# Attention with layers woven into it: three resident images, more buffers, later sums, depthwise taps through ScalarE, full-array projections

## The chip, the cores and the metric

One core of a Trainium2 chip. The metric is the device time of one execution in microseconds (us), as the median of the runs. The kernel before takes 3923 us. Here single runs of one kernel agree within 0.25%, and where a ratio is given it comes from three or more rounds in which both kernels ran on the same chip. The experiments ran in four batches on different chips; the kernel before had medians from 3921.2 to 3924.0 us in them, so a few us between runs of different batches mean nothing.

Engines are named as in the profile: PE is TensorE, PEld its weight loads, DVE is VectorE, ACT is ScalarE, POOL is GpSimd, SP is SyncE. "L643" is line 643 of the kernel named.

## The reference, cut to what matters

Four images of 256 channels and 48x48 points pass through four layers. Each layer is added to its input and works on the group norm of it. The attention of layer 0 (8 heads) and layer 2 (one head) over all 2304 points is most of the work.

```python
# layer 0: attention with normed q and k; the norm runs over the points
q, k, v = split(einsum('oc,bchw->bohw', w_qkv, x))       # 8 heads of 64
q = l2norm_over_points(q); k = l2norm_over_points(k)
attn = softmax(einsum('bhdi,bhdj->bhij', q, k) * 10.0)   # 2304 x 2304 a head
out = w_out @ einsum('bhij,bhdj->bhid', attn, v) + b_out

# layer 1: a gate from a depthwise filter on a 16 x 16 grid
t = blur_pool(max_pool_3x3(x), stride=3)                 # 48x48 -> 16x16
s = dwconv(t, w_h1) + dwconv(t, w_v1) + diag1(t, w_h2) + diag2(t, w_v2)   # 81 different taps
out = x * upsample(sigmoid(batch_norm(s)))

# layer 2: a non-local block with 64 channels
f = einsum('bnc,bcm->bnm', theta(x), phi(x)) * 64 ** -0.5
out = batch_norm_over_the_batch(W @ einsum('bnm,bmc->bnc', softmax(f), g(x)))

# layer 3: channel gates, depthwise 3x3, instance norm, leaky relu
x = x + layer_i(group_norm(x))                           # for each of the four
```

## The kernel before

The scores are worked out transposed: 128 keys on the partitions (a key block), 384 queries (a slice) of two heads beside each other. A **unit** is one slice of two heads: 18 key blocks in nine **groups** of two. A **stretch** is one pair of heads of one image in layer 0: six units, 54 groups; in layer 2 a stretch is one image: three units, 27 groups. There are 16 stretches and then four.

```python
    ppool = main.enter_context(tc.tile_pool(name="pt", bufs=5))      # exponentials
    apool = main.enter_context(tc.tile_pool(name="acc", bufs=2))
    hpool = main.enter_context(tc.tile_pool(name="half", bufs=2))    # half sums and rows
    ...
    def quarters(outs, lhsT, rhs, start, stop):      # four 64x64 matmuls for one 128x128
        for c in HALVES:
            for r, out in zip(HALVES, outs):
                nc.tensor.matmul(out[c], lhsT=lhsT[r, c], rhs=rhs[r], start=start, stop=stop)

    def join(out, ab, bias):                         # adds the two halves of the rows
        nc.scalar.activation(out, ab[0], AF.Identity, bias=bias)
        nc.vector.tensor_add(out, ab[1], out)

    def scores(u, j):
        ps = sc_tile()
        ...                                          # four matmuls of 64x64 on 384 columns
        pt = ppool.tile([P, 2, SL], F32, tag="pt", name="pt")
        nc.scalar.activation(pt, ps[:, :, :SL], AF.Exp, scale=u["scale"])

    def add_up(u, g):                                # softmax sums over the key blocks
        pts = [u["pt"][j] for j in range(g * G, (g + 1) * G)]
        if g in u["paired"]:                         # some groups: POOL adds the two blocks first
            half = hpool.tile([P, 2, SL], F32, tag="half", name="half")
            nc.gpsimd.tensor_add(half, pts[0], pts[1])
        ...
        for term in ready:
            nc.vector.tensor_add(u["acc"], u["acc"], term)

    def total(u):                                    # sums over the 128 partitions of acc
        ab = [pj_tile()[:, :SL] for _ in range(2)]
        ...                                          # four matmuls of ones with u["acc"]
        row = hpool.tile([P, 2, SL], F32, tag="half", name="row")
        for i in range(2):
            nc.scalar.copy(row[:, i, :], ab[i])
        ...                                          # DMA of the row to other partitions

    # groups from a unit's end until its sums, fold, 1/sum, division, and what follows
    AT_TOTAL, AT_FOLD, AT_INVERT, AT_DIVIDE, AT_AFTER = 1, 2, 4, 8, 11
```

The loop gives each engine its instructions in this order, group by group. Every engine works through its own list in order.

```python
        for t, (u, g, st) in enumerate(groups):
            for j in range(g * G, (g + 1) * G):
                scores(u, j)                # matmuls, and the exponentials of ACT
            if prev is not None:
                add_up(*prev)
            do(due, t)
            do(fills, t)                    # projections of the next pair, total(), outputs
            for lane in st["others"]:
                ...                         # the next "ticks" of layer 1 and of the group norms
            if prev is not None:
                ...                         # weigh(): attention times v for the group before
                if pg == NG - 1:
                    last(pu, t)             # copies the unit's result, enters its work in due, fills
```

Layer 1 of an image is a generator cut into ticks by `yield`; image 3's runs beside layer 2.

```python
        for i, (dr, dc) in enumerate(TAPS):          # 81 taps, three a tick
            ...
            nc.vector.scalar_tensor_tensor(acc, src, w, acc, ALU.mult, ALU.add)
            if i % TAPS_A_TICK == TAPS_A_TICK - 1 or i == len(TAPS) - 1:
                yield
    ...
        if b > 0:                                    # layer 2, image b, 27 groups
            spread(work, stats(b - 1, 1), [2, 3])    # two matmuls into two pj buffers each,
            spread(work, stats(b - 1, 2), [11, 12])  # then bn_stats by DVE
        if b + 1 < B:
            spread(work, stats(b, 0), [20, 21])
```

Small PSUM results all go through two buffers, called pj.

## Time and profile before

| | us |
|---|---|
| time, median of 4 runs (3918.99 to 3924.59) | 3923.0 |
| profiled execution | 3922.4 |
| prologue, to the first exponential | 74.1 |
| four stretches without layer 1 beside them (177.3 to 181.3 each) | 719.4 |
| twelve stretches with layer 1 (189.4 to 200.6 each) | 2337.2 |
| layer 2, first three images (135.5, 140.2, 168.5) | 444.2 |
| layer 2's last image and the tail | 347.2 |

A stretch is taken from the copy of the pair's last raw result (the product of attention and v, copied out of PSUM) to the next such copy; bounds are good to some 0.5 us (the first exponential starts at 74.4 us). These are groups of the kernel before (line, engine, operation, operands, count, then busy us and mean ns of one, then idle time before them):

```profile
L285 DVE TENSOR_TENSOR acc<-acc,pt 128x768 f32<-128x768 f32 x792 | 941.9, 1189 | 62.5 <-ACT pt L245 1.9
L643 DVE SCALAR_TENSOR_TENSOR l1acc<-pd,grid,l1acc 128x256 f32<-128x256 f32 x640 | 464.3, 726 | 16.4
```

And these are its waits over the whole run (what waited, for what, us in total, times, longest):

```profile
PEld pj L292 <- DVE acc L285: 144.4, 93, 7.8
PE pj L292 <- DVE acc L285: 98.7, 65, 6.9
ACT pt L245 <- DVE acc L285: 46.2, 42, 3.3
ACT pt L245 <- DVE acc L279: 18.7, 23, 2.3
```

104 units take their sums in this way; at 93 of them the weight load of the sums stood waiting for DVE's additions, and PE itself waited 98.7 us there. PE's next longest wait, of the scores for ACT, is 32.5 us in sum.

### The profile page before, as it was taken

Reading aid. Unit: us, or ns where it says so; the run is one execution under the profiler, and the core shown is the slowest. Engines: PE = TensorE matmul, PEld = TensorE weight load, DVE = VectorE, ACT = ScalarE, POOL = GpSimd, SP = SyncE. Lnnn points to the kernel's source line nnn. Section 1 sums busy time; section 2 is a strip of 40 time slices with the busy share of each in tenths; the row PEclk is TensorE's granted clock in tenths of the full one; section 3 lists DMA queues with packets and bytes.
Section 4 is the critical chain, followed back from the end, with each engine's and each line's share of the span. In section 5 each row is a group of like instructions: output and inputs, shape, how many; then the busy total and the mean of one; then the engine's idle time right before and its main releaser. Section 6 shows DMA issues by size and latency. Waiting matters only on the chain.

```text
span 3922.4 us, 91105 instructions
## 1 busy us (share of the span) xinstructions
PE 3595.0 (92%) x38642; PEld 1743.8 (44%) x38642; DVE 2947.4 (75%) x3799; ACT 2119.7 (54%) x3317; POOL 1450.9 (37%) x874
## 2 busy tenths in 40 slices
PE   6999999999989999999899999999999997869785
PEld 3444444444444444444444444444444443324343
DVE  2566555568987897689888976897888778874687
ACT  3656565656555555555565555555655543434353
POOL 1333333334333333343343333334433454553232
PEclk9999999999999999999999999999999998889897
DMA  4111111111111111111111111111110000000001
GB/s 149 20 28 21 25 20 28 19 27 24 20 17 26 17 27 23 20 24 20 20 24 20 23 24 20 24 20 24 20 16 8 8 4 5 5 5 5 1 25 73
DMA packets 109872, 91.10 MB, mean 23 GB/s; under 512 B 56096, under 2 KB 106896, under 8 KB 107664
## 3 DMA queue, kind: packets, MB, share of 16 engines
q1 hardware_dynamic: 106688, 84.06, 11.9%
q8 instruction: 305, 5.00, 0.5%
q10 hardware_dynamic: 2768, 1.14, 0.1%
q14 instruction: 111, 0.91, 0.1%
HBM read 54.62 MB, written 9.44 MB: 16 GB/s over the span
## 4 chain that ended last, share of the span: by engine, by line
PE 54%; DVE 33%; issue 6%; ACT 4%; POOL 3%; DMA 1%; SPq 0%; DVEq 0%; ACTq 0%; POOLq 0%
PE av L259 18%; PE sc L239 18%; DVE acc L285 14%; DVE l1acc L643 6%; PE pj L226 6%; PE pj L527 3%; PE pj L497 3%; PE pj L292 2%; DVE sc L1086 2%; POOL half L270 1%; DVE av L1086 1%; ACT pt L245 1%; DVE gn_st L168 1%; ACT k L229 1%; DVE k L230 1%
## 5 line engine op out<-in xcount | busy, mean ns | idle before, releaser
L245 ACT ACTIVATE pt<-sc 128x768 f32<-128x768 f32 x1944 | 1482.6, 809 | 1099.7 <-PE sc L239 936.9
L270 POOL TENSOR_TENSOR half<-pt 128x768 f32<-128x768 f32 x477 | 978.1, 2051 | 2098.7 <-ACT pt L245 1891.4
L239 PE MATMUL sc<-q,k 64*64 64x384 f32 x13824 | 1291.2, 486 | 17.3 <-ACT pt L245 15.0
L259 PE MATMUL av<-pt,v 64*64 64x384 f32 x13824 | 1299.2, 488 | 4.7 <-ACT raw L328 4.7
L285 DVE TENSOR_TENSOR acc<-acc,pt 128x768 f32<-128x768 f32 x792 | 941.9, 1189 | 62.5 <-ACT pt L245 1.9
L239 PEld LDWEIGHTS sc<-q,k 64*64 64x64 f32 x13824 | 529.3, 134 | 625.3 <-issue 521.7
L259 PEld LDWEIGHTS av<-pt,v 64*64 64x64 f32 x13824 | 522.5, 134 | 609.1 <-issue 593.8
L285 DVE TENSOR_TENSOR acc<-acc,half 128x768 f32<-128x768 f32 x459 | 480.6, 1047 | 68.5 <-POOL half L270 65.5
L643 DVE SCALAR_TENSOR_TENSOR l1acc<-pd,grid,l1acc 128x256 f32<-128x256 f32 x640 | 464.3, 726 | 16.4
L531 DVE SCALAR_TENSOR_TENSOR x<-pj,bo,x 128x384 f32<-128x384 f32 x192 | 118.5, 617 | 265.9 <-PE pj L527 265.4
L226 PE MATMUL pj<-xs,w 64*64 64x384 f32 x3072 | 292.5, 488 | 5.7 <-ACT q L229 4.1
L239 PE MATMUL sc<-qv,kd 64*64 64x384 f32 x1728 | 189.8, 505 | 17.7 <-ACT pt L245 17.6
L259 PE MATMUL av<-pt,qv 64*64 64x384 f32 x1728 | 199.5, 525 | 6.6 <-ACT raw L328 6.6
L292 PE MATMUL pj<-acc,ones 64*64 64x384 f32 x832 | 97.5, 529 | 99.6 <-DVE acc L285 98.7
L226 PEld LDWEIGHTS pj<-xs,w 64*64 64x64 f32 x3072 | 119.2, 134 | 142.9 <-issue 126.5
L527 PE MATMUL pj<-o,wo 128*128 128x384 f32 x384 | 158.8, 517 | 18.5 <-DVE bias L460 11.0
L497 PEld LDWEIGHTS pj<-w,xs 128*128 128x128 f32 x1152 | 137.1, 193 | 54.3 <-issue 42.4
L497 PE MATMUL pj<-w,xs 128*128 128x128 f32 x1152 | 155.1, 285 | 4.0 <-ACT k L229 4.0
L230 DVE TENSOR_TENSOR k<-pj,k 128x384 f32<-128x384 f32 x96 | 53.3, 555 | 139.5 <-ACT k L229 137.4
L336 POOL TENSOR_TENSOR o<-o,rinv 128x384 f32<-128x384 f32 x95 | 137.9, 1451 | 0.0
L230 DVE TENSOR_TENSOR q<-pj,q 128x384 f32<-128x384 f32 x96 | 53.4, 557 | 111.0 <-ACT q L229 111.0
L239 PEld LDWEIGHTS sc<-qv,kd 64*64 64x64 f32 x1728 | 79.4, 139 | 96.7 <-issue 54.7
(207 smaller groups left out, 2759.9 us busy)
## 6 DMA issues: line engine op xcount, KB each, us to landing
xs<-in_x_dram SPq DMA_DIRECT2D x96, 384.0 KB, 3.1
rinv<-rinv SPq DMA_DIRECT2D x208, 94.5 KB
x<-in_x_dram SPq DMA_DIRECT2D x8, 1152.0 KB, 5.5
out_dram<-x SPq DMA_DIRECT2D x6, 1152.0 KB, 4.3
l<-row SPq DMA_DIRECT2D x416, 1.5 KB, 1.8
w<-in_wqkv_dram SPq DMA_DIRECT2D x32, 192.0 KB, 6.7
rinv<-ls SPq DMA_DIRECT2D x208, 1.5 KB, 1.7
out_dram<-x SPq DMA_DIRECT2D x6, 384.0 KB, 2.6
```

The lines of the kernel that those rows point to most:

```text
L226: nc.tensor.matmul(out[c], lhsT=lhsT[r, c], rhs=rhs[r], start=start, stop=stop)
L230: nc.vector.tensor_add(out, ab[1], out)
L239: nc.tensor.matmul(ps[c * D : (c + 1) * D, h, :SL], lhsT=u["of"]["k"][r, j0 : j0 + D], rhs=u["of"]["q"][r, u["qc"]], start=True, stop=True,)
L245: nc.scalar.activation(pt, ps[:, :, :SL], AF.Exp, scale=u["scale"])
L259: nc.tensor.matmul(u["av"][h * D : (h + 1) * D, half, :SL], lhsT=value(u, j, h)[r], rhs=pt[r, h, :], start=j == 0, stop=j == JB - 1,)
L270: nc.gpsimd.tensor_add(half, pts[0], pts[1])
L285: nc.vector.tensor_add(u["acc"], u["acc"], term)
L292: nc.tensor.matmul(out[c], lhsT=ones[r], rhs=u["acc"][r, h, :], start=True, stop=True)
L336: eng.tensor_mul(o, o, u["rinv"])
L497: nc.tensor.matmul(ps[:, i * P : (i + 1) * P], lhsT=xs[s][:, k, i * P : (i + 1) * P], rhs=at["w"][:, k, 2, :], start=k == 0, stop=k == NK - 1,
L527: nc.tensor.matmul(ps[:, :SL], lhsT=wo[:, p, k * P : (k + 1) * P], rhs=o, start=True, stop=True)
L643: nc.vector.scalar_tensor_tensor(acc, src, w, acc, ALU.mult, ALU.add)
```

## The change

Its intent: take the waits for DVE off PE's path. Six things are done together.

- Ten buffers of exponentials instead of five, and three of half sums instead of two. The room comes from holding three images on the chip instead of four: image 3 takes the tile of image 0, which is written to DRAM and fetched back for layer 2's projection and for the tail.
- The sums of a unit are taken three groups after its end instead of one, and what follows moves with them.
- Layer 1's 81 taps: ACT makes the products, DVE adds up to five of them in one reduction.
- q, k and layer 2's theta and phi are projected with 128 rows and columns at once, so no join; q, k and v of a slice come in one group.
- Weights and norms of the next pair are fetched and made earlier.
- 48 small border copies of layer 1 move from ACT to DVE (`nc.scalar.copy` becomes `nc.vector.tensor_copy`; those after the normalising stay on ACT), and a few more ticks stand before steps that cross to another engine.

The diff, cut to its core:

```diff
-    X = [xpool.tile([P, NK, N], F32, tag=f"x{b}", name=f"x{b}") for b in range(B)]
+    NX = B - 1
+    X = [xpool.tile([P, NK, N], F32, tag=f"x{b}", name=f"x{b}") for b in range(NX)]
+    X.append(X[0])
+    x_out = dram.tile([P, NK, N], F32, name="x_out")
...
-    ppool = main.enter_context(tc.tile_pool(name="pt", bufs=5))
+    ppool = main.enter_context(tc.tile_pool(name="pt", bufs=10))
-    hpool = main.enter_context(tc.tile_pool(name="half", bufs=2))
+    hpool = main.enter_context(tc.tile_pool(name="half", bufs=3))
...
-    AT_TOTAL, AT_FOLD, AT_INVERT, AT_DIVIDE, AT_AFTER = 1, 2, 4, 8, 11
+    AT_TOTAL, AT_FOLD, AT_INVERT, AT_DIVIDE, AT_AFTER = 3, 2, 6, 10, 11
...
         def qk(s, t):
-            ab = [pj_tile()[:, :SL] for _ in range(2)]
+            ps = pj_tile()[:, :SL]
             for k in range(NK):
-                quarters(ab, at["w"][:, k, t, :], xs[s][:, k, :], k == 0, k == NK - 1)
-            join(to[:, cols], ab, at["bias"][:, t : t + 1])
+                nc.tensor.matmul(
+                    ps, lhsT=at["w"][:, k, t, :], rhs=xs[s][:, k, :],
+                    start=k == 0, stop=k == NK - 1,
+                )
+            nc.scalar.activation(to, ps, AF.Identity, bias=at["bias"][:, t : t + 1])
...
-    TAPS_A_TICK = 3
-    L1_TICKS = 2 * 8 + -(-len(TAPS) // TAPS_A_TICK) + 1 + 3
+    NT = 4
+    ROUNDS = [range(0, NT + 1)] + [
+        range(i, min(i + NT, len(TAPS))) for i in range(NT + 1, len(TAPS), NT)
+    ]
+    L1_TICKS = 2 * 10 + 2 * len(ROUNDS) + 2 + 3
...
+        bufs = [
+            lp.tile([P, L1_BUF], F32, tag=tag, name="prod").rearrange("p (n s) -> p n s", s=NT + 1)
+            for tag in ("t1", "t2")
+        ]
+        def products(n):
+            for i, t in enumerate(ROUNDS[n]):
+                ...
+                nc.scalar.activation(
+                    bufs[n % 2][:, :, min(n, 1) + i].rearrange("p (r c) -> p r c", c=AS),
+                    pd[:, PAD + dr : PAD + dr + AS, PAD + dc : PAD + dc + AS],
+                    AF.Identity, scale=grid[:, k, g : g + 1],
+                )
+        products(0)
+        yield
+        for n, taps in enumerate(ROUNDS):
+            last = n == len(ROUNDS) - 1
+            if not last:
+                products(n + 1)
+                yield
+            to = acc.rearrange("p r c -> p (r c)") if last else bufs[(n + 1) % 2][:, :, 0]
+            nc.vector.tensor_reduce(
+                to, bufs[n % 2][:, :, : min(n, 1) + len(taps)], AX.X, ALU.add
+            )
+            yield
...
+        if (b, p) == (2, 0):
+            for s in range(NSL):
+                work.setdefault(s, []).append(lambda s=s: send(s))         # image 0 to DRAM
+                work.setdefault(s + 8, []).append(lambda s=s: receive(s))  # image 3 into its tile
```

Note the product's place: `p (n s)` with `s` the five summands, so the five terms of one point lie beside each other, and ACT writes every fifth element, **20 bytes apart**. Layer 1 of an image has 146 ticks instead of 110.

## The prediction

> **What bounds the kernel now.** I read the page first. TensorE (PE) is busy for 92% of the span, so at first sight nothing but fewer matmuls can help. But the chain that ended last gives a third of the span to VectorE (DVE):
>
> ```profile
> PE 3595.0 (92%) x38642; PEld 1743.8 (44%) x38642; DVE 2947.4 (75%) x3799; ACT 2119.7 (54%) x3317; POOL 1450.9 (37%) x874
> PE 54%; DVE 33%; issue 6%; ACT 4%; POOL 3%; DMA 1%; SPq 0%; DVEq 0%; ACTq 0%; POOLq 0%
> ```
>
> So I cut the span into stages: the prologue; 16 attention stretches of layer 0 (one pair of heads of one image: 6 units of 9 groups of 2 key blocks); four of layer 2 (27 groups); the tail. The table of busy time by stretch (bounds in us, length, then PE, PEld, DVE, ACT, POOL, granted clock) has:
>
> ```profile
> 432.70:613.40 180.70, 179.72 (x2088) 88.21 (x2084) 106.07 (x134) 108.97 (x171) 59.90 (x37) 1.00 0.14 24
> 985.10:1185.70 200.60, 185.53 (x2092) 88.93 (x2088) 177.45 (x230) 110.44 (x173) 74.80 (x42) 0.98 0.13 21
> 3266.20:3406.50 140.30, 114.41 (x1142) 56.71 (x1138) 120.18 (x153) 59.20 (x95) 72.03 (x40) 0.91 0.06 6
> ```
>
> The first four stretches of layer 0 have no layer-1 work beside them and take 177.3 to 181.3 us. In the second of these lines PE is busy in 179.7 of 180.7 us, with a sixteen-instruction block starting every 1.29 us: PE-bound, nothing to win. The twelve stretches with layer 1 beside them take 189.4 to 200.6 us, **2337 us in all, some 170 more than twelve times 180.6**. Layer 2's first three take 135.5, 140.3 and 168.5 us, **444 us**, while the fourth, with no layer 1 and no projection, takes 80.5. So about 170 us are lost in layer 0 and some 150 in layer 2. The waits inside 985 to 1186 us (us, times, longest) name the loss:
>
> ```profile
> PEld pj L292 <- DVE acc L285: 16.6, 6, 5.4
> PE pj L292 <- DVE acc L285: 12.6, 6, 4.7
> ACT pt L245 <- DVE acc L285: 9.1, 6, 3.3
> ```
>
> The matmul of a unit's softmax sums (L292) stands one group after the unit's end and waits for DVE's last additions, 13 us of the 20 lost; and exponentials wait for one of five buffers that DVE has not yet read. DVE is late because of the layer-1 taps, and these are slow whenever GpSimd (POOL) works:
>
> ```profile
> 3278.70 3.85 DVE L643 SCALAR_TENSOR_TENSOR l1acc<-pd,grid,l1acc 128x256 f32<-128x256 f32 x3
> ...
> 3277.99 3.76 POOL L270 TENSOR_TENSOR half<-pt 128x768 f32<-128x768 f32 x2 [2.86 <-DVE acc L279]
> ```
>
> Three taps take 3.85 us here; the median tap takes 485 ns, so three should take 1.5. I sorted all taps of layer 0's stretches by whether a POOL instruction overlapped: 482 ns without, 1363 ns with.
>
> **What the Trainium skill says.** "SBUF — State Buffer", section "SBUF: two separate sides": VectorE and GpSimd share one pair of ports under an exclusive lock, taken by a GpSimd operation and by a VectorE one with two SBUF inputs or in a two-port mode. The trace agrees: taps and additions stretch under POOL; additions with one operand in PSUM (555 ns) and BN statistics (539 ns) don't. "VectorE: DVE Perf Modes", section "The perf-mode tier table", gives tensor_reduce only the 1x rate; the trace's reduction of 128x384 (0.55 us) agrees, and with one SBUF input it should not need the lock. "TensorE: Matmul & The Clock Gate", part 1: matmuls run at half clock until some 3.4 us of sustained work. In the prologue they are at half pace, with gaps, until about 36 us; that is longer. "TensorEngine Tiling (Array Packing)", "Key Properties": changing the tiling mode drains the array. Here entering a block of full-array matmuls costs 0.11 us and leaving it some 0.25 us (the first values after it), and before as after there is one such block per unit.
>
> **The shared ports as a budget.** I count instructions times their duration alone. In 985 to 1186 us: 79 additions of 0.95 us, 72 taps of 0.485 and 3 us of small ones make 113 us of DVE; 24 halves of 1.81, twelve 1.0, three 1.6 and small ones make 62 us of POOL: **175 of 200.6 us**. The same sum for 3266 to 3406 is 136 of 140; for the stretches without layer 1, 134 of 180.
>
> **The change, part by part.**
>
> *Taps.* Per image and half of the channels 81 taps leave DVE. ACT makes 81 products of 128x256 (0.5 us: ACT's 128x256 exponential at L651 takes 507 ns), in 20 rounds; DVE adds a round with one reduction of 256x5 elements. From 0.55 us for 384 elements, about 0.15 us fixed and 1.04 ns each: 1.48 us, 30 us for 20, against 39 us alone and 58 us as measured. All 39 us leave the ports' budget: eight times 39 is 310 us. ACT gains eight times 40, at 54% busy.
>
> *Joins.* Full-array projections drop 240 additions of 0.555 us on DVE (133 us), and with them PSUM buffers that waited for DVE. On PE nothing changes: four 64x64 matmul instructions start 4 x 80.6 = 322 ns apart, a full-array one of 128x384 also 322.
>
> *Buffers and slots.* Ten buffers instead of five let exponentials run on while DVE and POOL are three groups late instead of half a group; sums three slots on give DVE two more groups (over 5 us) before L292, more than most of those waits; a third half-sum buffer lets POOL go on while the row of sums is being sent.
>
> *x in three tiles* only makes the room. It adds twelve DMAs of 384 KB in a stretch where DMA is 13% busy, fetches for layer 2's first projection, and a reload at the tail that is used last. I charge nothing.
>
> Sums, before to after:
> - Prologue, 74.1: a warm slice takes 7.14 us because every projection waits for its eviction and join. PE work is 12 x 0.112 + 8 x 0.322 = 3.9, so about 4.1. Start at 24.0, 12 us at half clock for 1.5 slices, 4.5 x 4.1 = 18.5, and 2.5 for scales: **57, so -17**.
> - Four stretches without layer 1, 719: **-3**.
> - Twelve with layer 1, 2337: port load falls to 140-157, PE's 180 is the bound again. I allow 2 us each for leftover waits (ACT makes four products, 2 us, in a group where PE needs 2.6 and the exponentials 1.5), and 177 for the last, which has the smaller layer-2 projection: 11 x 182 + 177 = 2179, **-158**.
> - Layer 2, three stretches, 444: three limits lie close. PE: 27 x 2.58 + 15 + 6 = 91 each, 273. Ports: 117, 136 and 124 less 76 of taps, 301. ACT in groups with taps: 1.5 + 1.8 + 0.45 of evictions = 3.75 a group for some 36 groups, 135, plus 45 groups of ports at 4.2/0.95, 199: 334. The last five groups of the third stretch now take 8.4 us each, as phi, theta and g wait in turn for two PSUM buffers; without joins some 6.2. With 10 us for that end: **344, -100**.
> - Last stretch and tail, 347.5: **-1**.
>
> Total -279: 3924 - 279 = **3645 us**.
>
> **Rivals.** (1) *ACT becomes the bound* in layer 2 and around the sums: a group with products, the raw copy and evictions needs 4.3 us of ACT against PE's 2.6. For it: 146 layer-1 ticks go into some 66 groups there. Against it: ACT was 40% busy in those stretches, and ten buffers average over groups. Then layer 2 takes 390 and each layer-1 stretch 185: 3725. (2) *PE was the bound all along*: 92% busy, the work of attention is unchanged, so only the prologue and joins pay; about 3860. Against it: the 180 against 200 us with the same PE instructions. (3) *Decoupling works fully*: all layer-1 stretches at 179, layer 2 at 310: 3570. Against it: port load stays at 78 to 87%. (4) *One lump per unit* of 5.2 us holds up DVE's residual additions and fills both PSUM buffers, 1 us a unit: +80 us. Against it: today's two-part block does the same at 0.1 us.
>
> **Range and chances.** The main doubt is layer 2 (310 to 390), then leftover waits in layer 0 (+-35). Together 3590 to 3710 should hold it 8 times in 10. A gain under 2% would need rival 2 or 4 with most of 1 to be true: faster 0.97, same 0.025, slower 0.005.
>
> **What would show it.** Right: the layer-1 stretches at 180 to 184 us with PE busy nearly throughout; no wait of L292 for acc; exponentials waiting only for scores; reductions at 1.4 to 1.5 us, with or without POOL; products at about 0.5 us; first scores near 57 us; layer 2 near 115, 115 and 120 us. Wrong: reductions that stretch under POOL, scores that wait for exponentials behind products, or a longer block per unit. The total is wrong above all if layer 2 stays above 400, or the layer-1 stretches above 187.

## The result, and the profile after

The kernel after takes **3766.2 us** (3764.58 to 3770.24, four runs), where 3645 (3590 to 3710) was predicted. The ratio is 0.9603 (95%: 0.9587 to 0.962). Ratios here are the mean time of one kernel's fast runs over the mean of the other's fast runs of the same rounds, so they are not quite the ratios of the medians. The direction was right, and the size was not: 157 us came of 279, and the time is outside the range.

| stage (us) | before | predicted | after |
|---|---|---|---|
| prologue | 74.1 | 57 | 55.2 |
| four stretches without layer 1 | 719.4 | 716 | 721.5 |
| twelve with layer 1 | 2337.2 | 2179 | **2237.6** |
| layer 2, first three images | 444.2 | 344 | **399.3** |
| layer 2's last image and tail | 347.2 | 346.5 | 348.9 |

So the shortfall lies in two stages, 59 us in the stretches with layer 1 and 55 in layer 2. In the page of the kernel after, the busy line and the chain answer to the two of before:

```profile
PE 3537.2 (94%) x35954; PEld 1769.4 (47%) x35954; DVE 2531.3 (67%) x3151; ACT 2421.5 (64%) x3913; POOL 1373.6 (37%) x874
PE 71%; DVE 14%; ACT 8%; issue 4%; POOL 2%; DMA 1%; SPq 0%; DVEq 0%; ACTq 0%; POOLq 0%
```

DVE's part of the chain fell from 33% to 14%; ACT's rose from 4% to 8%, and its busy time by 302 us. The stretches (bounds, length, busy time of PE, PEld, DVE, ACT, POOL, granted clock, DMA share, GB/s) show where PE still stands idle. The first has no layer 1, the second has, the third is layer 2's second image:

```profile
415.70:596.20 180.50, 179.71 (x1944) 90.15 (x1939) 93.39 (x123) 108.70 (x171) 59.05 (x37) 1.00 0.14 24
963.50:1153.50 190.00, 184.03 (x1948) 88.03 (x1944) 136.34 (x164) 139.13 (x232) 65.61 (x42) 1.00 0.14 22
3143.50:3276.20 132.70, 108.94 (x1056) 52.00 (x1056) 104.71 (x98) 92.43 (x160) 73.88 (x43) 0.93 0.06 6
```

DVE's load in the second line fell from 177 to 136 us, and yet the stretch takes 190. The waits inside that stretch, for comparison with the three lines that the prediction shows of it:

```profile
PEld sc L234 <- ACT pt L240: 11.6, 20, 0.8
PE av L254 <- ACT raw L323: 2.5, 2, 1.3
```

The waits for `acc` are gone, of the sums and of the exponentials: none is among the sixty longest of the whole run. PE now waits for ACT, which comes late to the exponentials that free the scores' PSUM buffers. These are ACT's products and DVE's reductions in the groups of the kernel after:

```profile
L666 ACT ACTIVATE prod<-pd,grid 128x256 f32<-128x256 f32 x648 | 373.9, 752 | 8.6 <-DVE prod L680 8.5
L680 DVE TENSOR_REDUCE prod<-prod 128x256 f32<-128x1280 f32 x152 | 224.9, 1480 | 14.2 <-ACT prod L666 14.1
```

The reduction takes 1480 ns as predicted; the product takes 752 ns in the mean (745 in the median), where 500 had been assumed. Products overlap, though: 648 of 752 ns would be 487 us, and ACT is busy with them for 373.9. In a row one starts 518 ns after the other (median), and four hold ACT for 2.3 us.

In layer 2 another kind of wait comes in. These are the waits from 3014 to 3414 us, which hold its first three images:

```profile
PEld av L254 <- ACT raw L323: 29.2, 9, 9.4
PEld pj L287 <- DVE bst L818: 17.2, 14, 4.5
ACT t L628 <- DVE t L624: 15.2, 2, 8.4
```

And this is the timeline of one long group there (start, length, engine, line; in brackets the idle time before and what ended it):

```profile
3220.86 2.00 POOL L265 TENSOR_TENSOR half<-pt 128x768 f32<-128x768 f32 x1 [3.17 <-ACT pt L240]
...
3221.11 1.80 DVE L609 COPY t<-x 128x26 f32<-128x26 f32 x1
...
3231.24 1.40 DVE L624 TENSOR_TENSOR t<-t 128x1200 f32<-128x1200 f32 x1
...
3232.74 1.39 ACT L628 ACTIVATE t<-t,gn_nb,gn_rs 128x1200 f32<-128x1200 f32 x1 [8.42 <-DVE t L624]
...
3234.31 0.79 ACT L323 COPY raw<-av 128x768 f32<-128x768 f32 x1
...
3235.15 2.20 PE L254 MATMUL av<-pt,qv 64*64 64x384 f32 x12 [8.70 <-ACT raw L323]
```

ACT's normalising of layer 1 (L628) stands at the head of ACT's list and waits 8.42 us for a maximum of DVE, which is late. Behind it in ACT's list are the unit's raw copy and the next exponentials, which wait for nothing but their turn, and PE waits 8.70 us for them. The kernel before has such waits too, but shorter: PE waited 6.6 us in sum for the raw copy in the same three images, 3.5 at the longest, where the kernel after has 24.6 and 8.7. Groups that take long for other reasons it had as well: the longest took 18 us before and 19 after.

The same timeline shows one reason why DVE is late. From 3219.8 us it works without a pause, and two of its instructions are border copies that the change moved to it, L609 (shown) and L612. They take 1.80 and 1.79 us, and each ends within 0.1 us of the end of a half sum of POOL. Over the whole run such copies (L609, L612, L618, L622) take 0.18 us when no POOL instruction overlaps them (33) and 1.3 us in the mean, 1.8 at most, when one does (15); on ACT, in the kernel before, they took 0.22 to 0.24. With L614 beside POOL (2.13 us, against 1.39 without) that is some 4 of the 8.42 us, by my estimate. No run puts the copies back.

### The profile page after: what moved, and what is told of

Same layout as the page of the kernel before. It is cut to its first block, busy times and chain, and to the rows that moved or that the text cites. A ratio compares the mean times of both kernels' runs of the same rounds, so it can differ in the third digit from the quotient of the medians.

```text
span 3762.8 us, 85538 instructions
## 1 busy us (share of the span) xinstructions
PE 3537.2 (94%) x35954; PEld 1769.4 (47%) x35954; DVE 2531.3 (67%) x3151; ACT 2421.5 (64%) x3913; POOL 1373.6 (37%) x874
## 4 chain that ended last, share of the span: by engine, by line
PE 71%; DVE 14%; ACT 8%; issue 4%; POOL 2%; DMA 1%; SPq 0%; DVEq 0%; ACTq 0%; POOLq 0%
PE av L254 27%; PE sc L234 26%; PE pj L483 6%; DVE acc L280 4%; PE pj L540 4%; PE pj L497 3%; ACT prod L666 3%; ACT pt L240 2%; DVE sc L1159 2%; PE pj L287 2%; DVE av L1159 1%; DVE x L706 1%; PE pj L752 1%; PE pj L780 1%; DVE z L1208 1%
## 5 line engine op out<-in xcount | busy, mean ns | idle before, releaser
L265 POOL TENSOR_TENSOR half<-pt 128x768 f32<-128x768 f32 x477 | 922.0, 1933 | 1704.0 <-ACT pt L240 1637.8
L280 DVE TENSOR_TENSOR acc<-acc,pt 128x768 f32<-128x768 f32 x792 | 892.7, 1127 | 92.8 <-ACT pt L240 9.8
L666 ACT ACTIVATE prod<-pd,grid 128x256 f32<-128x256 f32 x648 | 373.9, 752 | 8.6 <-DVE prod L680 8.5
L483 PE MATMUL pj<-xs,w 128*128 128x384 f32 x768 | 266.4, 489 | 5.0 <-ACT v L502 4.9
L331 POOL TENSOR_TENSOR o<-o,rinv 128x384 f32<-128x384 f32 x95 | 124.1, 1306 | 331.0 <-DMA rinv<-rinv 296.0
L680 DVE TENSOR_REDUCE prod<-prod 128x256 f32<-128x1280 f32 x152 | 224.9, 1480 | 14.2 <-ACT prod L666 14.1
L254 PE MATMUL av<-pt,qv 64*64 64x384 f32 x1728 | 185.1, 512 | 24.6 <-ACT raw L323 24.6
L483 PEld LDWEIGHTS pj<-xs,w 128*128 128x128 f32 x768 | 138.6, 191 | 84.1 <-ACT v L502 11.8
L274 DVE TENSOR_TENSOR acc<-pt 128x768 f32<-128x768 f32 x99 | 119.2, 1204 | 10.7 <-ACT pt L240 10.6
L254 PEld LDWEIGHTS av<-pt,qv 64*64 64x64 f32 x1728 | 76.2, 138 | 94.4 <-issue 55.4
```

The lines of the kernel that those rows point to most:

```text
L254: nc.tensor.matmul(u["av"][h * D : (h + 1) * D, half, :SL], lhsT=value(u, j, h)[r], rhs=pt[r, h, :], start=j == 0, stop=j == JB - 1,)
L274: nc.vector.tensor_add(u["acc"], ready[0], ready[1])
L331: eng.tensor_mul(o, o, u["rinv"])
L483: nc.tensor.matmul(ps, lhsT=at["w"][:, k, t, :], rhs=xs[s][:, k, :], start=k == 0, stop=k == NK - 1,)
L666: nc.scalar.activation(bufs[n % 2][:, :, min(n, 1) + i].rearrange("p (r c) -> p r c", c=AS), pd[:, PAD + dr : PAD + dr + AS, PAD + dc : PA ...
L680: nc.vector.tensor_reduce(to, bufs[n % 2][:, :, : min(n, 1) + len(taps)], AX.X, ALU.add)
```

## The experiments

Three theories were set against each other. **Shared ports**: DVE's and POOL's work on their common ports is the bound beside layer 1, and the move of the taps to ACT earns the time. **ScalarE**: products in groups where ACT also has exponentials and evictions make ACT the bound. **Decoupling and order**: what counts is how late one engine may be before another stops for it; buffers and later sums earn the time, and an instruction at the head of a list that waits for late work costs it. All runs were timed in rounds against the kernel before; sums of stretches are from the profile ("L1" the twelve with layer 1, "L2" layer 2's first three images). All results are correct unless it says otherwise. Edits are against the kernel after unless it says otherwise.

| run | median us | ratio to before (95%) | L1 | L2 |
|---|---|---|---|---|
| before | 3923.0 | 1 | 2337.2 | 444.2 |
| after | 3766.2 | 0.9603 (0.9587-0.962) | 2237.6 | 399.3 |
| e1_contig | 3786.4 | 0.965 (0.9634-0.9666) | 2251.7 | 407.9 |
| e2_taps_on_dve | 3737.2 | 0.9528 (0.9512-0.9544) | 2202.7 | 405.0 |
| e3_five_pt | 3810.4 | 0.9715 (0.9699-0.9731) | 2283.7 | 398.0 |
| e4_slots_back | 3895.9 | 0.9931 (0.9914-0.9947) | 2377.8 | 388.8 |
| e5_norm_on_dve | 3753.5 | 0.9571 (0.9555-0.9587) | 2226.7 | 398.0 |
| e6_taps_norm_dve | 3736.1 | 0.9529 (0.9513-0.9545) | 2199.7 | 405.1 |
| e7_both_unstepped | 3723.9 | 0.9498 (0.9482-0.9514) | 2208.6 | 384.2 |
| e8_five_pt_slots_back | 3845.3 | 0.9805 (0.9789-0.9822) | 2328.1 | 389.5 |
| e9_stats_later | 3748.0 | 0.9558 (0.9542-0.9574) | 2237.5 | 388.6 |
| e10_norm_dve_stats_later | 3737.0 | 0.9528 (0.9512-0.9544) | 2227.6 | 385.1 |
| e11_hybrid | 3713.8 | 0.9472 (0.9457-0.9488) | 2199.7 | 386.5 |
| e12_before_sums_later | 3936.0 | 1.0034 (1.0017-1.0051) | 2357.4 | 430.5 |
| e13_idle_products | 3705.6 | 0.9449 (0.9433-0.9464) | 2203.2 | 377.9 |
| e14_idle_both | 3708.6 | 0.9459 (0.9443-0.9474) | 2199.9 | 378.6 |
| e15_changed_spaced | 3739.4 | 0.9535 (0.9519-0.9551) | 2239.2 | 374.7 |

### The taps: e1, e2, e7

**e1_contig** writes each product in one piece, so that ACT's writes have no step, and the reduction's reads get one of 1024 bytes.

```diff
-            lp.tile([P, L1_BUF], ...).rearrange("p (n s) -> p n s", s=NT + 1)
+            lp.tile([P, L1_BUF], ...).rearrange("p (s n) -> p n s", s=NT + 1)
```

> Layer 1's products are written tap after tap (each product 256 elements in a row) instead of five products interleaved with a step of 20 bytes; the reduction on VectorE then reads with a step of 1024 bytes. Theory: the product's 745 ns (I had taken 507 from another 128x256 activation) come from the interleaved writes. Then a product takes about 507 ns, a group with products in layer 2 falls from some 3.85 us to about 3.2, and if the reduction stays at 1.48 us the total falls by 30 to 60 us (3705 to 3735). Rival: they come from the reading of 16 of 28 columns or from the per-partition scale; then products stay at 745 ns and the total within 10 us of 3766. If the reduction is slowed by its stepped reads, its duration shows it (over 2 us) and the gain is smaller.

Measured, the groups of this kernel:

```profile
L680 DVE TENSOR_REDUCE prod<-prod 128x256 f32<-128x1280 f32 x152 | 368.4, 2424 | 6.9 <-ACT prod L666 6.2
L666 ACT ACTIVATE prod<-pd,grid 128x256 f32<-128x256 f32 x648 | 280.6, 512 | 55.0 <-DVE prod L680 54.5 <-ACT pt L240 0.2
```

The product falls from 752 to 512 ns and the reduction rises from 1480 to 2424: the step costs whichever side has it. ACT is freed of 93 us and DVE gets 144 more, ACT's products now wait 54.5 us for the reductions, and the kernel is 20 us slower. So the layout chosen in the change is the better of the two, and by itself this run doesn't tell what the products' length costs. That is the next one's question.

**e7_both_unstepped** gives both sides their short form. The products are written in one piece and the reduction reads neighbouring elements, so it adds the wrong ones: the result is wrong (relative error 0.253). The reduction takes the maximum, so that nothing grows without bound; its length is the same, 1478 ns.

```diff
-                    bufs[n % 2][:, :, min(n, 1) + i].rearrange("p (r c) -> p r c", c=AS),
+                    flat[n % 2][:, (min(n, 1) + i) * AS * AS :][:, : AS * AS].rearrange(...),
...
-            to = ... if last else bufs[(n + 1) % 2][:, :, 0]
+            to = ... if last else flat[(n + 1) % 2][:, : AS * AS]
...
-                to, bufs[n % 2][:, :, : min(n, 1) + len(taps)], AX.X, ALU.add
+                to, bufs[n % 2][:, :, : min(n, 1) + len(taps)], AX.X, ALU.max
```

> A wrong result on purpose: products are written tap after tap (as in the run with stepped reads), and the reduction reads the same buffer in order, five neighbours at a time, with max in place of add so that nothing grows without bound. So both the product (512 ns) and the reduction (1.48 us) are as short as my prediction took them. If the product's size was the term that failed, the total falls to about 3700 (layer-1 stretches of layer 0 near 2200, layer 2 near 370). If ScalarE's place in the chain matters and not the length of its products, it stays above 3750.

Measured, the products of this kernel:

```profile
L664 ACT ACTIVATE prod<-pd,grid 128x256 f32<-128x256 f32 x648 | 280.5, 514 | 11.8 <-DVE prod L678 11.6
```

They take 514 ns, and the kernel 3723.9 us: **42 us less** than the kernel after, 29 of them in the stretches with layer 1 and 15 in layer 2. The 648 products keep ACT busy for 280.5 us instead of 373.9, so 42 of 93 us reach the end. In layer 2 the 35 groups that hold products take 147 us together instead of 162, which is the whole gain there; in the kernel after ACT is busy for over 95% of the time in 27 of the 35. At least 79 us of the shortfall have other causes.

**e2_taps_on_dve** leaves all of the change but the taps, which stay on DVE, three a tick, as before.

```diff
-        products(0)
-        ...                                  # products and reductions in 20 rounds
+        for i, (dr, dc) in enumerate(TAPS):
+            ...
+                nc.vector.scalar_tensor_tensor(acc, src, w, acc, ALU.mult, ALU.add)
+            if i % TAPS_A_TICK == TAPS_A_TICK - 1 or i == len(TAPS) - 1:
+                yield
```

> The changed kernel with layer 1's 81 taps back on VectorE, three a tick as before; everything else of the change stays. If moving the taps is what pays, layer 2's first three stretches return to about 440 us (from 399) and the twelve layer-1 stretches of layer 0 to about 2290 (from 2238): total 3850 to 3870. If the buffers, the later sums and the missing joins are what pay, the total is 3765 to 3800. My guess is 3820.

Measured: 3737.2 us, **29 us faster than with the taps on ACT**: 35 less in the stretches with layer 1, 6 more in layer 2. Two stretches of this run, the one without taps and the one with:

```profile
777.80:959.30 181.50, 180.71 (x1948) 90.59 (x1944) 134.21 (x170) 112.19 (x178) 67.13 (x40) 1.00 0.13 20
959.30:1144.50 185.20, 182.14 (x1948) 90.44 (x1944) 168.15 (x223) 109.10 (x172) 72.46 (x41) 0.99 0.15 23
```

And the taps of the second one:

```profile
L665 DVE SCALAR_TENSOR_TENSOR l1acc<-pd,grid,l1acc 128x256 f32<-128x256 f32 x78 | 54.0, 692 | 1.9
```

This is the run that overturns the budget. By the prediction's own count the second stretch carries 78 additions of 0.95 us, 78 taps of 0.485 and 3 us of small ones on DVE, 115 us, and 61 of POOL: 176 of its 185 us, 95%. The taps are as slow as ever, 692 ns. And PE is busy in 182.1 of 185.2 us. A load of 95%, so counted, goes with some 4 us more than the stretch without taps takes, where 87% went with a loss of 20 in the kernel before: the count by itself sets no bound. That it does little harm as long as no one has to wait for a particular piece of it at once is my reading; the waits below speak for it.

### Buffers and slots: e3, e4, e8, e12

**e3_five_pt**: five buffers of exponentials again. **e4_slots_back**: the sums one group after the unit again, with ten buffers. **e8_five_pt_slots_back**: both. **e12_before_sums_later**: the kernel before, with the later slots alone.

```diff
 e3, e8
-    ppool = main.enter_context(tc.tile_pool(name="pt", bufs=10))
+    ppool = main.enter_context(tc.tile_pool(name="pt", bufs=5))
 e4, e8 (e12 does the reverse in the kernel before)
-    AT_TOTAL, AT_FOLD, AT_INVERT, AT_DIVIDE, AT_AFTER = 3, 2, 6, 10, 11
+    AT_TOTAL, AT_FOLD, AT_INVERT, AT_DIVIDE, AT_AFTER = 1, 2, 4, 8, 11
```

> The changed kernel with five buffers of exponentials instead of ten. If decoupling by buffers is a main cause of the gain, the layer-1 stretches of layer 0 rise by 4 us each or more and layer 2 by 30 us: total 3840 or more. If with fewer VectorE operations five were enough, within 15 us of 3766. My guess is 3830.

> The changed kernel with the sums one group after a unit's end instead of three (and inverse and division two groups earlier too). If the wait of the matmul of the sums for VectorE was what the layer-1 stretches lost, it comes back there: plus 3 to 6 us in each of twelve, total 3800 to 3840. In layer 2 the sums would no longer share a group with the statistics of the layer-2 output, which use the same two PSUM buffers: if that collision costs there, layer 2's three stretches fall by 10 to 30 us.

> The changed kernel with five buffers of exponentials and the sums one group after the unit's end: both of these parts undone. Five buffers alone cost 44 us, the earlier sums alone 130. If they add, 3940, slower than the kernel before. If ten buffers are what lets VectorE fall so far behind that early sums wait longer, this is no slower than with the earlier sums alone: 3850 to 3896. My guess is 3870.

> The kernel before with the one line of constants alone: sums three groups after a unit's end, inverse at six, division at ten. In the changed kernel with five buffers these constants were worth 35 us (3845 to 3810), with ten 130 us. If in the kernel before the wait of the sums for VectorE is what the layer-1 stretches lose (13 of 20 us in one of them), these fall by 5 to 10 us each and the total to 3820 to 3860. If with five buffers and the taps, joins and sums all on VectorE something else ends the waiting, about 3890. My guess is 3870.

With the rest of the change in place, the four kernels make a square (us):

| | sums one group on | sums three groups on |
|---|---|---|
| five buffers | 3845 (e8) | 3810 (e3) |
| ten buffers | 3896 (e4) | 3766 (after) |

**The two parts don't add.** Later sums with five buffers gain 35 us, ten buffers with early sums *lose* 51, and together they gain 79. The waits over the whole run say why. With ten buffers and early sums (e4):

```profile
PE pj L287 <- DVE acc L280: 126.9, 36, 6.8
```

With five buffers and early sums (e8):

```profile
ACT pt L240 <- DVE acc L280: 87.1, 73, 3.5
PE pj L287 <- DVE acc L280: 52.9, 32, 4.5
```

With five buffers and late sums (e3), where the wait of L287 for `acc` is no longer among the 60 longest:

```profile
ACT pt L240 <- DVE acc L280: 56.9, 57, 3.8
ACT pt L240 <- DVE acc L274: 34.6, 11, 6.1
```

Few buffers hold DVE close, because exponentials stop when DVE is late; then the sums find their additions nearly done. With more buffers DVE may fall further back, and the early sums stop PE outright: 127 us instead of 53. With late sums and few buffers the exponentials are what stops. Only both together leave no wait for `acc` among the 60 longest.

e12 shows the same in the kernel before, and it was 13 us *slower* (1.0034, the interval just clear of 1). Its waits over the whole run, beside the four of before:

```profile
ACT pt L245 <- DVE acc L279: 60.0, 24, 4.5
ACT pt L245 <- DVE acc L285: 55.5, 66, 3.9
```

The waits of the sums for `acc` have left the list of the 60 longest and the waits of the exponentials went from 65 to 116 us: +20 us in the stretches with layer 1, -14 in layer 2. The wait that one takes away is made good by the next that stands behind it.

The square also splits the gain of the whole change. From before to e8, which has all of it but these buffers and slots, 78 us are gained: 20 in the prologue, 9 in the stretches with layer 1, 55 in layer 2, less 5 in the stretches without. In layer 2 the taps' move can be some 6 of the 55 (e2); that the rest comes from the missing joins is likely, but no run puts these back. Nor does any run undo the third half-sum buffer, the three tiles or the earlier fetches by itself. From e8 to after, buffers and slots gain 79: 90 in the stretches with layer 1, and a *loss* of 10 in layer 2. That loss is the next question.

### Layer 2: e9, e15

A unit of layer 2 ends with groups 8, 17 and 26 of an image, its last work is issued at slots 9, 18 and 0, and with the sums three slots on they are taken at 12, 21 and 3. At just these slots stand layer 2's statistics (2, 3, 11, 12, 20, 21). Both take two pj buffers, of which there are two, and the statistics free theirs only when DVE has come to them. **e9_stats_later** moves the statistics.

```diff
-            spread(work, stats(b - 1, 1), [2, 3])
-            spread(work, stats(b - 1, 2), [11, 12])
+            spread(work, stats(b - 1, 1), [5, 6])
+            spread(work, stats(b - 1, 2), [14, 15])
...
-            spread(work, stats(b, 0), [20, 21])
+            spread(work, stats(b, 0), [23, 24])
...
-            slots = [s for s in range(n) if s not in (1, 2, 3, 10, 11, 12, 19, 20, 21)]
+            slots = [s for s in range(n) if s not in (3, 5, 6, 12, 14, 15, 21, 23, 24)]
```

> The changed kernel with the statistics of layer 2's output three groups later, so that they no longer share a group, and the two PSUM buffers, with the sums that the change moved onto them. If that collision is what the changed slots cost in layer 2 (389 us with the old slots, 399 with the new), the three stretches fall by 10 us or more, total about 3755. If not, within 5 us of 3766.

Measured: 3748.0 us, 18 less than the kernel after; layer 2 falls from 399.3 to 388.6 us, where it was with the old slots (389 in e4 and e8). The sums' wait for the statistics (17.2 us above) is gone from this stage. So the collision cost 11 us there. The rest is spread: 2.5 us lie in layer 2's last image, whose statistics moved too, and 1 to 2 each in the prologue and the tail, which the edit doesn't touch.

**e15_changed_spaced** adds to e9 five empty ticks for the last image, whose layer 1 runs beside layer 2, ahead of three instructions that need DVE's work of the tick before: the normalising activation, the first products, and the first matmul of the group norm. DVE then has more groups to finish what they wait for.

```diff
+            for _ in range(IDLE if b == B - 1 else 0):
+                yield                              # ahead of the normalising activation
...
+        for _ in range(IDLE if b == B - 1 else 0):
+            yield                                  # ahead of products(0)
...
+        for _ in range(idle):
+            yield                                  # in gn, ahead of its first matmul
```

> The changed kernel, engines as the change has them, with the statistics three groups later and five idle ticks before each cross-engine step of layer 1's last image (normalising, first products, matmul of the group norm). If distance is what counts in layer 2, its three stretches fall from 399 to about 360 and the total to about 3728. If normalising on ScalarE costs by its place, 385 or more.

Measured: 3739.4 us; layer 2 takes 374.7 us, **14 less than e9**, with no arithmetic taken away or made shorter, and 35 ticks more. The stretches with layer 1 are as in e9 (2239.2 against 2237.5), as they should be, since no tick of theirs was moved.

### Who should do which part: e5, e6, e10, e11, e13, e14

**e5_norm_on_dve** gives DVE layer 1's normalising, the two border copies that had stayed on ACT and the factor 1/64, so that this chain crosses to ACT no more until the products. **e6_taps_norm_dve** does the same with e2's taps on DVE. **e10_norm_dve_stats_later** is e5 with e9's slots.

```diff
-            nc.scalar.activation(
-                t2[:, r:25, 1:49], t2[:, r:25, 1:49], AF.Identity,
-                bias=norm["nb"][:, k : k + 1], scale=norm["rs"][:, k : k + 1],
+            nc.vector.tensor_scalar(
+                t2[:, r:25, 1:49], t2[:, r:25, 1:49], norm["rs"][:, k : k + 1],
+                norm["nb"][:, k : k + 1], ALU.mult, ALU.add,
             )
```

> The changed kernel with layer 1's normalising of the pooled rows, its two border copies and the scaling by 1/64 on VectorE instead of ScalarE, so that no exponential stands in ScalarE's queue behind an instruction that waits for VectorE's maxima. If that waiting in order makes the long groups of layer 2 (8 to 19 us), layer 2's three stretches fall by 20 to 40 us and the total to about 3730. If the shared ports are what those groups wait for, nothing is gained (VectorE gets some 20 us more work under the lock): 3760 to 3780.

> As the run with the taps on VectorE, and the normalising there too: layer 1 leaves ScalarE but for its gate's exponential. If waiting in order on ScalarE makes the long groups, layer 2's three stretches fall from 405 to about 370 and the total to about 3700. If VectorE and its ports are then the bound, 3735 or more.

> The changed kernel with both: layer 1's normalising on VectorE and the statistics three groups later. Normalising alone gave layer 2 one us, though groups waited 8.4 us for it: the wait may only have been passed on to the two PSUM buffers. If so, both together give more than the sum of each alone: layer 2's three stretches at 370 or less, total about 3725. If the ports bound them, 390 or more.

Measured: e5 gains 13 us on the kernel after, 11 of them in the stretches with layer 1; layer 2, where the long waits are, gains 1. e10 gains 11 on e9. With the taps on DVE, e6 gains nothing that the interval can show over e2 (3736.1 and 3737.2). In e6's trace the wait in layer 2 has only changed its owner: PE's matmuls of the statistics stand 4.98 us for BN statistics that DVE does behind eleven taps, and ACT's copy of the sums stands 10.97 us behind PE.

**e11_hybrid** takes the better side of each stage: e10, with the taps on DVE for the three images beside layer 0 and on ACT for the last one beside layer 2.

```diff
+        if b < B - 1:
+            for i, (dr, dc) in enumerate(TAPS):
+                ...                               # taps on DVE as in e2
+        else:
+            ...                                   # products and reductions as in the change
```

> The run before this one with the taps on VectorE for the three images whose layer 1 runs beside layer 0, and on ScalarE for the last, beside layer 2. Layer 0's layer-1 stretches should be those of the run with taps on VectorE (2200), layer 2 that of the run before this one: total about 3690 to 3700. If layer 2 isn't helped, 3725.

Measured: 3713.8 us, 52 less than the kernel after; 2199.7 us in the stretches with layer 1, the best with e6. Layer 2 keeps a wait that e5's edit handed on, as this timeline of e11 shows:

```profile
3060.55 0.26 DVE L655 TENSOR_SCALAR pd<-tf 128x128 f32<-128x128 f32 x1
...
3060.90 2.77 ACT L682 ACTIVATE prod<-pd,grid 128x256 f32<-128x256 f32 x5 [12.69 <-DVE pd L655]
...
3063.47 0.84 ACT L323 COPY raw<-av 128x768 f32<-128x768 f32 x1
3064.36 2.84 PE L254 MATMUL av<-pt,qv 64*64 64x384 f32 x16 [12.55 <-ACT raw L323]
```

ACT waits no more for the maximum, but its first products now wait 12.69 us for the factor 1/64, and again PE stands behind the raw copy.

**e13_idle_products** adds five empty ticks ahead of these products for the last image; **e14_idle_both** also five ahead of the group norm's first matmul, which had waited 12.74 us in the kernel after.

```diff
+            for _ in range(IDLE):
+                yield
             products(0)
```

> The hybrid with five idle ticks (some two groups) between layer 1's pooled rows and the first products of the last image. If the 18.6 and 15.4 us groups are ScalarE waiting in order, both fall to about 5 us and layer 2's three stretches from 386 to about 365; total about 3692. If VectorE is simply late there, the wait only moves on: 380 or more.

> The same, and five idle ticks between the statistics and the first matmul of the last group norm, which now stands for 12.7 us at the head of TensorE's queue. If distance ends it, the 19.8 us group falls to about 8 and the total by another 10 us: about 3680. If the idle ticks only make the other ticks denser, no change from the run before.

Measured: e13 takes **3705.6 us**, the fastest of all, 5.5% under the kernel before; layer 2 falls from 386.5 to 377.9 us and the group of 18.6 us that held the wait is gone. The intervals of e11 and e13 overlap, so only the trace, not the time, makes the difference sure. e14 gained nothing more (3708.6, within the intervals): the group norm's wait is gone, but a copy of the sums' row then waits 14.6 us for DVE's additions in one unit. Groups of 16.2 and 20.7 us stay in e13, and of 16.7 and 16.9 in e14, where the median group takes 4.2. Which instruction is caught at the head of a list changes with each shift, and I found no placement without one.

## Why the prediction was wrong, point by point

**The product of ACT: the first failed step.** The step "81 products of 128x256 (0.5 us: ACT's 128x256 exponential at L651 takes 507 ns)" took its duration from an instruction that writes neighbouring elements. The change writes every fifth, and this takes 752 ns. As products overlap, four of them hold ACT for 2.3 us where the prediction reckoned 2 (1.8 in layer 2), and all for 374 us where it reckoned 8 x 40 = 320. e1 shows 512 for the same instruction without the step, and e7 shows what the difference is worth: 42 of the 121 us between 3645 and 3766, 29 in layer 0's stretches and 15 in layer 2. In e7 four products hold ACT for 1.73 us, less than the prediction reckoned, so 42 us is the most that the wrong size can have cost; in proportion to ACT's time, (374 - 320) / (374 - 281), it would be some 24, an estimate. With longer products the rival "ACT becomes the bound" came true in groups that have them: in layer 2 most of these take 3.5 to 4.3 us, and ACT is busy nearly throughout in 27 of 35. Its totals were 390 for layer 2 and 185 for a stretch; measured were 399 and 186.5.

**The shared ports as a budget: the wrong cause.** The prediction counted 175 of 200.6 us on the shared ports, concluded that taps must leave them, and had 310 us of such load removed. The slowing of taps under POOL is real (692 ns in e2, 485 alone), but a 95% load was carried in e2 with PE busy in 182 of 185 us. The ports still matter in another way, as a delay and not as a sum: small copies of DVE that stand 1.8 us under POOL make DVE late for those who wait for it. The taps' move, which the prediction took for the heart of the change, cost 29 us net; with both forms short e7 is some 12 us faster than e2 (0.9498 against 0.9528, the intervals touch; 21 less in layer 2, 6 more beside layer 0), so with short products the move would have paid a little. What earned the time beside layer 1 was the pair of buffers and slots, 90 us by e8. The prediction named this part too and called the waits of L292 "13 us of the 20 lost", but put the cure in the taps.

**Stretches with layer 1: 2179 predicted, 2237.6 measured.** Of the 59 us, the products' step is 29 at most (e7), the taps' move as a whole 35 (e2), and normalising on ACT 11 (e5; these overlap and are not to be added). The best versions come to 2200, or 183.3 a stretch, where the prediction allowed 182. In them PE itself is busy for some 2 us longer than in stretches without layer 1 (182.1 against 180.7 in e2); why, stays open. The 2 us a stretch of leftover waits were thus about right for a version that the change is not.

**Layer 2: 344 predicted, 399.3 measured; the second failed step.** The prediction added up engine loads and held that "ten buffers average over groups". Two things were not in the sum. First, the collision of the moved sums with the statistics on the two pj buffers, 11 us (e9). The slot numbers were in the diff: 9 + 3 = 12 against a statistic at 12. Second, instructions that stand at the head of ACT's or PE's list and wait 8 to 13 us for late DVE work: spacing them out was worth 14 us (e15), and 9 in e13. I had taken these waits for the price of the ten buffers, which let DVE be later. The square refutes that for layer 2: ten buffers or five make no difference there (388.8 and 389.5 with early sums, 399.3 and 398.0 with late ones), and the wait of L628 is as long with five (8.5 us at the longest in e3, 8.0 in e8). DVE's copies under POOL are some 4 us of one such wait, by the timeline above; the rest of its lateness is not settled. With the products' 15 us, that is some 40 of the 55 us, if they add, which no run tested at once. **The remaining 15 or so stay open**; the best layer 2 of all runs took 374.7 us, 31 over the estimate. The estimate itself, ports for 199 us and ACT for 135, stands on the budget that e2 has overturned, so it is no floor.

**Stretches without layer 1**: -3 predicted, +2 measured, of 719. The removed joins freed DVE, which was not the bound there, and nothing was to be had.

**What held.** The prologue: 57 predicted, 55.2 measured, in part by luck: the matmuls came to full pace before 30.8 us and not at 36, so the slices ended at 50.4 and not at 54.5, but from there to the first exponential it took 5.1 us and not 2.5. A slice takes 3.92 us instead of 7.14, by the timeline of PE in the kernel after:

```profile
30.78 1.50 PE L497 MATMUL pj<-w,xs 128*128 128x128 f32 x12
32.11 2.75 PE L483 MATMUL pj<-xs,w 128*128 128x384 f32 x8
34.70 1.50 PE L497 MATMUL pj<-w,xs 128*128 128x128 f32 x12
```

From 30.78 to 34.70 are 3.92 us, where 3.9 was worked out. The reduction: 1.48 us predicted, 1480 ns measured, and sorted by whether a POOL instruction overlapped, 1480 with and 1478 without, so it doesn't wait for POOL. The waits of the sums for `acc` are gone. The rival "PE was the bound all along" (3860) and the lump per unit (+80 us) are both out: 3766, and stretches without layer 1 that changed by 2 us in four. The rival of full decoupling (3570) fell with layer 2.

The general mistake was one of confidence: the doubt was put into layer 2 (310 to 390) and leftover waits, and neither term for an instruction whose access pattern had no example in the trace nor one for waiting in order was given room. Rival 1's sum, 3725, was outside the range that followed from it, and the truth lay 41 us beyond.

## What to carry to other kernels

When a buffer ring and a fixed slot both hold back the same late engine, loosen both and measure them together: here the ring alone cost 51 us, since the engine fell further behind and the slot then cost more, and the slot alone handed its wait to the ring, with a gain of 35 us in one kernel and a loss of 13 in the other. When slots move, write down which others take the same small buffers at the new slots, and look at each instruction that follows the work of another engine by a fixed step, since it holds up everything behind it in its list; spacing such steps cost nothing that shows in e13 and e15. When small instructions change engines, look in the trace at what else that engine must wait for: 0.18 us alone was up to 1.8 under POOL. Before moving work to another engine, find in the trace an instruction of the same engine **with the same step in its output**, or take the duration as unknown; and where instructions overlap, take busy time and not durations.

## What the Trainium skill lacked or had wrong

- "SBUF — State Buffer", the note on SBUF cachelines in the section "Door 1: The DMA port swizzle (why `[64,N]` ≈ `[32,N]`)": 16-byte lines, with at least two hits a line needed for full speed. It would have warned of the first failed step, and the runs agree in direction: 752 ns for a product whose 256 elements are written 20 bytes apart against 512 side by side, and 2424 ns for a reduction that reads 1280 elements 1024 bytes apart against 1480. But it gives no cost for ACT or DVE; here it is (2424 - 1480) / 1280 = 0.74 ns an element for DVE's reads, and for ACT's writes (752 - 512) / 256 = 0.94 ns in the length of one product, though only (518 - 409) / 256 = 0.43 ns in the time from one start to the next.
- No page that I read tells how to reckon what an instruction at the head of an engine's in-order list costs the work behind it while it waits for another engine: single waits of 8.4 to 14.6 us here, in groups of 4.2 in the median, and 14 us of layer 2 gained by spacing alone.
